# Six PSUM banks for the last attention unit, and another order of loads in the output projection of a conditioned transformer block

## The chip, the cores and the metric

The kernel runs on one core of a Trainium2 chip (trn2). The metric is the device time of one execution in microseconds; smaller is better. Of several runs the median is given. One further execution was profiled, and every time that is placed on an axis here is counted from the start of that profile's span.

## The reference

A transformer block whose normalisations are modulated by a condition vector: x is (2, 2048, 512) in float32, 16 heads of 32, a hidden layer of 2048.

```python
mod = silu(condition) @ Wada + bada
sh_a, sc_a, gt_a, sh_m, sc_m, gt_m = split(mod, 6, axis=1)
xm = layernorm(x, g1, be1) * (1 + sc_a) + sh_a
q, k, v = split_heads(xm @ Wqkv)                    # 16 heads of 32
a = softmax(where(causal, q @ k.T * 32**-0.5, -inf)) @ v
x = x + gt_a * (merge_heads(a) @ Wproj + bproj)
xm = layernorm(x, g2, be2) * (1 + sc_m) + sh_m
x = x + gt_m * (gelu(xm @ W1 + b1) @ W2 + b2)       # exact gelu
```

## The kernel before

The two batches are worked one after the other: modulation, query/key/value products of batch 0, attention of batch 0, output projection of batch 0, query/key/value products of batch 1, attention of batch 1, output projection of batch 1, and last the two-layer perceptron of both batches.

**Attention** goes by units. A unit is a group c of four heads (C is 4 groups) and a block i of 512 queries; a batch has 16 units, and the order of the blocks in the last group is 0, 2, 1, 3 (`last_order`), so the last unit has the most keys. A unit is cut into steps, one for each tile of 128 keys (the last three tiles under the causal mask, which are narrower, share two steps); the last unit has 15 steps. In a step, for each of the four heads:

- TensorE puts minus the row maxima into a PSUM bank (`st`, from `fold` and `sel`), the four heads side by side, and adds the transposed scores (`st`, from `qst` and `kst`); a bank comes from `st_bank()`;
- ScalarE takes the exponential out of the bank into SBUF (`e`, L566), and with that the bank is free;
- two steps later TensorE multiplies `e` by the values (`o`); sums over keys are made by adding pairs and fours of `e` (`ee`, L592, on VectorE in the last unit and on GpSimd otherwise) and by a product with ones (`sm`).

PSUM has eight banks: two of the pool `ps_s` (tag "s": row maxima, gate row and the scores of later units), four of `ps_st` (tag "st"), and one each for `o` and `sm`. In the last unit no later scores are left, so `st_bank` counts its banks (`n_bank`) and takes one in six from "s". In the last unit `prepare` also works ahead for the projection: at step 5 it makes the row of the gate in an "s" bank (`ps_rows`) and copies it to SBUF (L406), then it multiplies the projection's weights and the first block of attention outputs. `prefetch` (step 3) loads the projection's weights, the first two blocks of outputs (`at_s`), the first four token tiles (`xt_s`) and the next stage's first tokens into SBUF that the keys and queries no longer need.

**The output projection** (`project_phase`) goes over 16 tiles of 128 tokens, four for each block in `last_order`; `n` counts them. For a tile:

- SyncE loads its tokens `xt` (L951; the first four are there already), and GpSimd adds the gated bias to them (L952);
- TensorE makes the tile's product over four chunks of 128 (`ps_o`; each chunk is two records in the profile, since they are float32);
- VectorE adds the product to `xt` (L959) and takes its statistics (L204, L205), SyncE stores it (L961);
- VectorE multiplies one chunk of the next block's outputs by their inverse softmax sums (L965), which TensorE needs for the next block's tiles.

The inverse sums come through DRAM: the sums are loaded (`load_sums`, L322), inverted on VectorE (`invert`, L329) and stored (L330), and then loaded spread over the partitions (`widen`, L336, into `wide_d` or straight into SBUF). For the last unit all of that can only be done in the projection. `rb` and `rbs` are the spread inverses, a block each.

Between the tiles, `between(n)` does work of the stage that follows: for batch 0 it loads the weights of the query/key/value products (`load_w`, L758, three transfers of 1 MB from ScalarE's queue) and normalises the first tokens of batch 1 (`norm`); for batch 1 it normalises and transposes tokens for the perceptron (`ln_t`) and adds them up (`token_sums`).

Each engine has a queue of its own and works it in order. A scheduler fills the queues by when it takes an instruction to be ready, earlier than the program's order where it can; `mm(...)` and `act(...)` pin an instruction behind all that was written before it for its engine. Transfers are not pinned. An SBUF pool opened after another was closed lies in the same memory, so its tiles wait until the old ones are done with.

Of the kernel before, what the change touches and what calls it, by code (L numbers as in the profile page):

```python
# [8 lines left out]
F32 = mybir.dt.float32  # L9
# [8 lines left out]
P = 128  # L18
# [3 lines left out]
QB = 512  # L22
# [5 lines left out]
def dit_block_kernel(  # L28
# [35 lines left out]
    nc = tc.nc  # L64
    B, T, D = x.shape
    HID = W1.shape[1]
    C = D // P
    FC = HID // P
    NT = T // P
    HC = P // HD  # L70
    TQ = QB // P
# [11 lines left out]
    def pool(name, bufs=1, **kw):  # L83
        return tc.tile_pool(name=name, bufs=bufs, reuse_waits="tile", **kw)
# [101 lines left out]
    def x_rows(n):  # L186
        t0 = (n % NT) * P
        return x[n // NT, t0 : t0 + P, :]

    def mm(*args, **kw):  # L190

        return tc.keep_in_program_order(nc.tensor.matmul(*args, **kw))  # L192

    def act(ins):

        return tc.keep_in_program_order(ins)
# [5 lines left out]
    def stats(pool_, xt, n, mv):  # L202
        st = pool_.tile([P, 6], F32, tag="stat", name="stat", bufs=2)
        nc.vector.bn_stats(st, xt)  # L204
        nc.vector.bn_aggr(mv[:, n, :], st)  # L205

    def inv_std(mv, rstd, lo, hi):
        nc.scalar.activation(rstd[:, lo:hi], mv[:, lo:hi, 1], AF.Sqrt, bias=eps)
        nc.vector.reciprocal(rstd[:, lo:hi], rstd[:, lo:hi])
# [50 lines left out]
    units = []  # L260
# [4 lines left out]
    last_order = [i for _, i in units[-NQ:]]  # L265
# [249 lines left out]
    def attention_phase(row):  # L515
        b, vv, kst, qst = row.b, row.vv, row.kst, row.qst
        with pool(f"att{b}") as ap, pool(
# [4 lines left out]
            n_bank = [0]  # L522

            def scores_t(u, step, n):

                def st_bank():

                    n_bank[0] += u == len(units) - 1
                    if n_bank[0] % 6 > HC:
                        return ps_sp.tile([P, QB], F32, tag="s", name="st")
                    return ps_stp.tile([P, QB], F32, tag="st", name="st")

                c, i = units[u]  # L540
                tiles = steps_of[u][step]
                q0 = tiles[0][1]
                w = sum(QB - q for _, q in tiles)
                sts, es = [], []
                row.score(max(0, n - 5))
                n = min(n, 5)
                for h in range(HC):
                    g = slice(h * HD, (h + 1) * HD)
                    st = st_bank()
                    mm(  # L550
                        st[:, :w], sel[g, :], fold[u % 2][g, q0 : q0 + w],
                        start=True, stop=False,
                    )
                    sts.append(st)
                for h in range(HC):
                    at = 0
                    for j, q in tiles:
                        mm(
                            sts[h][:, at : at + QB - q],
                            kst[c][:, h, j * P : (j + 1) * P],  # L560
                            qst[u][:, h, q:],
                            start=False, stop=at + QB - q == w,
                        )
                        at += QB - q
                    e = ap.tile([P, QB], F32, tag="e", name="e", bufs=E_BUFS)
                    act(nc.scalar.activation(e[:, :w], sts[h][:, :w], AF.Exp))  # L566
                    if tiles[0][0] >= i * TQ:

                        d = e.rearrange("p (t k) -> p t k", k=P)[:, 0 : TQ : TQ - 1, :]
                        d = d[:, : len(tiles), :]  # L570
                        act(
                            nc.gpsimd.affine_select(  # L572
                                d, d, pattern=[[0, len(tiles)], [1, P]],
                                compare_op=ALU.is_ge, fill=0.0,
                                base=0, channel_multiplier=-1,
                            )
                        )
                    es.append(e)
                    if h >= HC - n:
                        row.score(1, st_bank if h == 2 else None)  # L580
                row.score(n - HC)
                return es
# [61 lines left out]
            def due(u, step):  # L644

                rate, past = 0.0, weight[step]
                for v in range(u + 1, len(units)):

                    left = sum(weight[step : max(step + 1, starts[v] - 3)])
                    rate = max(rate, (cum[v] - row.spent) / left)  # L650
                return row.spent + rate * past

            for u, (c, i) in enumerate(units):
# [5 lines left out]
                for n_step, tiles in enumerate(steps_of[u]):  # L659
                    last = n_step == steps - 1  # L660
                    if n_step == 0:
# [4 lines left out]
                    n = row.count(  # L666
                        due(u, starts[u] + n_step) - QB // 2, u + AHEAD
                    )
# [70 lines left out]
    class Qkv:  # L739
# [20 lines left out]
        def norm(self, g, j):  # L760
# [12 lines left out]
            )  # L773

        def group(self, g, hp, between, among):


# [138 lines left out]
    def project_phase(row, psum, between):  # L916

        b = row.b
        with pool(f"proj{b}") as pp:
            n = 0
            ats = list(row.at_s)
            rbs = {1: row.rb_s[1], 2: row.old_queries()}
            for k, i in enumerate(last_order):
                if k in (0, 1):

                    at = pp.tile([P, C, QB], F32, tag="at", name="at", bufs=2)
                    nc.sync.dma_start(at, od[b][last_order[k + 2]])  # L930
                    ats.append(at)
                at = ats[k]
                for t in range(TQ):

                    if n == 0:
                        rbs[3] = pp.tile([P, C, QB], F32, tag="rb", name="rb")
                        row.load_sums(len(units) - 1, len(units))
                        nc.sync.dma_start(rbs[2], wide_d[b][last_order[2]])
                    elif n == 1:
                        row.invert(len(units) - 1, len(units))  # L940
                        nc.sync.dma_start(
                            rbs[3][:, : C - 1], wide_d[b][last_order[3]][:, : C - 1]
                        )
                    elif n == 2:
                        row.widen(len(units) - 1, rbs[3][:, C - 1, :])
                    nt = b * NT + i * TQ + t
                    if k == 0:
                        xt = row.xt_s[t]
                    else:
                        xt = pp.tile([P, D], F32, tag="xt", name="xt", bufs=4)  # L950
                        nc.sync.dma_start(xt, x_rows(nt))  # L951
                    act(nc.gpsimd.tensor_tensor(xt, xt, bgate, ALU.add))  # L952
                    ps = psum.tile([P, D], F32, tag="mm", name="ps_o")
                    for c in range(C):
                        mm(
                            ps, at[:, c, t * P : (t + 1) * P], row.wproj[:, c, :],
                            start=(c == 0), stop=(c == C - 1),
                        )
                    nc.vector.tensor_tensor(xt, ps, xt, ALU.add)  # L959
                    stats(pp, xt, nt, mv2)  # L960
                    nc.sync.dma_start(x1d[nt], xt)  # L961
                    if k + 1 < NQ:
                        d = ats[k + 1][:, t, :]
                        act(
                            nc.vector.tensor_tensor(d, d, rbs[k + 1][:, t, :], ALU.mult)  # L965
                        )
                    between(n)
                    n += 1
        inv_std(mv2, rstd2, b * NT, (b + 1) * NT)


    row = Row(0)
# [115 lines left out]
    first, row = row, Row(1)  # L1088
    with pool("qkv1") as qp, pool("ps_qkv1", bufs=6, space=PSUM) as ps_mm:
        qkv = Qkv(row, qp, ps_mm)  # L1090
        qkv.xts[0] = first.next_s

        def between(n):
            if n == 2:
                qkv.load_w(nc.scalar)
            if n in (5, 8):
                qkv.norm(0, n // 8)()

        project_phase(first, ps_mm, between)

        def also(g, n):
            if n % 4 == 1:
                quarters.step()

        with pool("hl1") as hp:
            quarters.more_rooms = lambda: [
                hp.tile([P, piece], F32, tag="w7", name="w7", bufs=2)
            ]
            qkv.run(hp, also)
            assert quarters.at >= FC  # L1110
            quarters.store()
# [8 lines left out]
    with ExitStack() as mlp:  # L1120
# [54 lines left out]
        def between(n):  # L1175
# [13 lines left out]
            if n == 13:  # L1189
                token_sums()  # L1190

        project_phase(row, ps_mm, between)
        w7 = [load_w1(f) for f in range(2)]
        bp_cm.__exit__(None, None, None)
# [270 lines left out]
```

## Time and profile before

| | |
|---|---|
| median of three runs | 2526.72 us (2524.92 to 2527.82) |
| the profiled execution | 2526.39 us, its span 2524.7 us |
| busy in the span | PE 2460.4, VectorE 1351.5, GpSimd 982.0, ScalarE 895.1 us |
| last unit of batch 0 (756.9 to 805.2) | 48.30 us, PE busy 48.11, granted clock 1.00 |
| projection of batch 0 (805.2 to 875.7) | 70.50 us, PE busy 61.27, granted clock 0.95 |
| last unit of batch 1 (1603.3 to 1651.6) | 48.30 us, PE busy 48.11, granted clock 1.00 |
| projection of batch 1 (1651.6 to 1713.3) | 61.70 us, PE busy 59.67, granted clock 1.00 |

PE is TensorE's products, PEld its weight loads, DVE is VectorE, ACT ScalarE, POOL GpSimd, SP SyncE; L959 is line 959 of the kernel. A product's end is modelled in the profile, so PE that counts as busy may still be waiting for a bank; the starts are measured, and differences from start to start are the safer reading. A line of a timeline has start, duration, engine, line, operation, what is written from what, tile shapes, count, and in brackets the idle time ahead of it with what ended it. A line of waits has total, times and longest. In both, the part before the colon or bracket names who waited and for what.

### The profile page before, as it was taken

How to read it: one execution, taken by the hardware profiler on the slowest of the kernel's cores; microseconds unless marked ns; L12 is line 12 of the kernel's file. 1: busy time of each engine (PE TensorE's matmuls, PEld its weight loads, DVE VectorE, ACT ScalarE, POOL GpSimd, SP SyncE). 2: the span in 40 equal slices, each digit the busy share in tenths (PEclk: the TensorE clock that was granted, in tenths of full speed). 3: DMA queues.
4: the chain of work that ended last, by engine and by line, in shares of the span. 5: the costliest groups of instructions: out<-in, count | busy, mean ns of one | idle time of the engine just before them, and what ended most of it. 6: DMA issues, size and time to landing. Idle time of an engine off the chain costs nothing.

```text
span 2524.7 us, 30931 instructions
## 1 busy us (share of the span) xinstructions
PE 2460.4 (97%) x10977; PEld 1172.8 (46%) x10977; DVE 1351.5 (54%) x2820; ACT 895.1 (35%) x1667; POOL 982.0 (39%) x1158
## 2 busy tenths in 40 slices
PE   7999999999999899999999999999999999999998
PEld 3445445444444344554444444444444444444443
DVE  3465657667565625656675756665353353344424
ACT  2213455454545011155545454613312312311310
POOL 0062786766772362058767785241101201200200
PEclk9999999999999999999999999999999999999999
DMA  6667123041224596450514113163223233322422
GB/s 221 208 223 193 39 52 84 22 109 43 87 90 141 193 296 200 133 109 22 109 43 93 39 38 134 68 219 119 87 92 132 85 100 108 108 93 72 140 84 96
DMA packets 133445, 285.71 MB, mean 113 GB/s; under 512 B 13301, under 2 KB 42525, under 8 KB 128426
## 3 DMA queue, kind: packets, MB, share of 16 engines
q1 hardware_dynamic: 126226, 257.47, 34.2%
q0 software_dynamic: 5376, 23.07, 2.6%
q10 hardware_dynamic: 1688, 3.19, 0.4%
q8 instruction: 86, 1.41, 0.2%
q14 instruction: 69, 0.57, 0.1%
HBM read 209.76 MB, written 81.79 MB: 115 GB/s over the span
## 4 chain that ended last, share of the span: by engine, by line
PE 61%; DVE 2%; DMA 1%; SPq 1%; issue 0%; ACT 0%; POOL 0%; DVEq 0%; ACTq 0%
PE ps_y L192 15%; PE ps_h L192 15%; PE st L192 9%; PE o L192 5%; PE s L192 4%; PE ps_qk L192 4%; PE ps_o L192 2%; PE sm L192 2%; PE ps_v L192 2%; SPq L336 1%; PE ps_xt L200 1%; DVE junk L436 1%; PE ps_o L200 0%; DVE mx L441 0%; DMA r<-sum 0%
## 5 line engine op out<-in xcount | busy, mean ns | idle before, releaser
L566 ACT ACTIVATE e<-st 128x512 f32<-128x512 f32 (+1 forms) x1152 | 575.3, 576 | 509.4 <-PE st L192 460.5
L441 DVE TENSOR_REDUCE mx<-s 128x1 f32<-128x512 f32 x616 | 413.7, 686 | 273.5 <-PE s L192 272.1
L592 POOL TENSOR_TENSOR ee<-e 128x512 f32<-128x512 f32 x336 | 420.9, 1287 | 246.3 <-ACT e L566 245.7
L192 PE MATMUL s<-kst,qst 128*128 128x512 f32 (+3 forms) x1058 | 453.5, 447 | 17.8 <-DVE mx L436 8.5
L192 PE MATMUL st<-qst,kst 128*128 128x512 f32 (+3 forms) x1280 | 438.1, 392 | 0.0
L192 PE MATMUL o<-e,vv 128*32 128x512 f32 (+3 forms) x2560 | 294.9, 542 | 0.0
L192 PE MATMUL ps_h<-sx,w 128*128 128x512 f32 x640 | 286.7, 592 | 0.0
L436 DVE CUSTOM_DVE_ANT_0 junk<-s,causal 128x384 bf16<-128x384 f32 (+3 forms) x442 | 211.1, 478 | 138.9 <-PE s L192 130.6
L1236 POOL TENSOR_TENSOR c<-c 128x512 f32<-128x512 f32 x32 | 40.6, 1270 | 620.9 <-DVE c L1198 620.9
L192 PE MATMUL ps_y<-sh,w 128*128 128x512 f32 x640 | 277.5, 593 | 0.0
L192 PEld LDWEIGHTS st<-qst,kst 128*128 128x128 f32 x1280 | 230.4, 192 | 88.0 <-issue 63.3
L192 PEld LDWEIGHTS s<-kst,qst 128*128 128x128 f32 x1058 | 199.3, 190 | 144.0 <-issue 47.7
L192 PE MATMUL ps_qk<-xmT,wqkv 128*128 128x512 f32 x512 | 242.3, 601 | 2.2 <-DVE xmT L248 2.2
L572 POOL TENSOR_SCALAR_AFFINE_SELECT e<-e 128x128 f32<-128x128 f32 (+1 forms) x384 | 124.3, 341 | 289.3 <-ACT e L566 282.8
L1198 DVE TENSOR_TENSOR h<-c,ps_h 128x512 f32<-128x512 f32 x128 | 88.0, 687 | 232.5 <-PE ps_h L192 232.5
L592 POOL TENSOR_TENSOR ee<-ee 128x512 f32<-128x512 f32 x168 | 210.8, 1283 | 0.0
L192 PEld LDWEIGHTS ps_h<-sx,w 128*128 128x128 f32 x640 | 121.1, 190 | 150.2 <-issue 149.5
L192 PEld LDWEIGHTS ps_y<-sh,w 128*128 128x128 f32 x640 | 121.1, 191 | 148.3 <-issue 146.9
L192 PE MATMUL st<-fold,sel 32*128 32x512 f32 (+1 forms) x1152 | 156.8, 485 | 2.7 <-DVE fold L500 2.0
L1222 ACT ACTIVATE h<-h,cols 128x512 f32<-128x512 f32 x128 | 92.3, 721 | 182.0 <-DVE h L1198 182.0
L192 PEld LDWEIGHTS st<-fold,sel 32*128 32x128 f32 x1152 | 62.2, 183 | 183.8 <-ACT e L566 124.8
L192 PEld LDWEIGHTS ps_qk<-xmT,wqkv 128*128 128x128 f32 x512 | 95.2, 192 | 98.9 <-issue 91.8
(124 smaller groups left out, 2368.9 us busy)
## 6 DMA issues: line engine op xcount, KB each, us to landing
qst<-q SPq DMA_DIRECT2D x128, 256.0 KB
w<-w1d SPq DMA_DIRECT2D x34, 896.0 KB
w<-w2d SPq DMA_DIRECT2D x28, 1024.0 KB
kst<-k SPq DMA_DIRECT2D x24, 1024.0 KB
q<-hl SPq DMA_DIRECT2D x32, 512.0 KB
k<-hl SPq DMA_DIRECT2D x32, 512.0 KB
kst<-k SPq DMA_DIRECT2D x32, 256.0 KB
w<-in_L_cond_W_dram POOLq DMA_DIRECT2D x64, 128.0 KB, 4.7
```

The costliest lines, as they stand in the source:

```text
L192: return tc.keep_in_program_order(nc.tensor.matmul(*args, **kw))
L200: return tc.keep_in_program_order(nc.tensor.transpose(dst, src, ident[:n, :n]))
L336: nc.sync.dma_start(dst, inv_d[self.b][u].unsqueeze(1).to_broadcast([HC, HD, QB]),)
L436: nc.vector.tensor_tensor_reduce(junk[:, :w], s[:, :w], causal[:, QB - w :], 1.0, MASKED, ALU.add, ALU.max, m,)
L441: nc.vector.tensor_reduce(m, s[:, :w], axis=AX.X, op=ALU.max)
L566: act(nc.scalar.activation(e[:, :w], sts[h][:, :w], AF.Exp))
L572: nc.gpsimd.affine_select(d, d, pattern=[[0, len(tiles)], [1, P]], compare_op=ALU.is_ge, fill=0.0, base=0, channel_multiplier=-1,)
L592: act(engine.tensor_tensor(dst, x, y, ALU.add))
L1198: nc.vector.tensor_tensor(dst, x, y, op)
L1222: nc.scalar.activation(d, d, AF.Gelu, bias=col(r_b1 + chunk, 1))
L1236: nc.gpsimd.tensor_tensor(c1_, c1_, c2_, ALU.subtract)
```

## The change

It has four edits. In `st_bank`, two of six banks of the last unit come from "s" instead of one of six, so that its tiles go round six banks. In `project_phase`, the tokens are loaded by `tokens(upto)` into six buffers instead of four: six tiles ahead of everything else in the phase, and then, at tile n, up to tile n + 5. The spread inverses of the last block go into the buffer of the first block's (`row.rb_s[0]`) instead of one of their own; their first three chunks are loaded at tile 0 instead of 1, the last unit's sums are inverted at tile 3 instead of 1 and spread at tile 4 instead of 2. In batch 0, `load_w` is called at tile 6 instead of 2.

```diff
                     n_bank[0] += u == len(units) - 1
-                    if n_bank[0] % 6 > HC:
+                    if n_bank[0] % 6 >= HC:
                         return ps_sp.tile([P, QB], F32, tag="s", name="st")
                     return ps_stp.tile([P, QB], F32, tag="st", name="st")
...
             n = 0
             ats = list(row.at_s)
-            rbs = {1: row.rb_s[1], 2: row.old_queries()}
+            rbs = {1: row.rb_s[1], 2: row.old_queries(), 3: row.rb_s[0]}
+            rows_x = [b * NT + i * TQ + t for i in last_order for t in range(TQ)]
+            xts = list(row.xt_s)
+
+            def tokens(upto):
+                while len(xts) < min(upto, NT):
+                    xt = pp.tile([P, D], F32, tag="xt", name="xt", bufs=6)
+                    nc.sync.dma_start(xt, x_rows(rows_x[len(xts)]))
+                    xts.append(xt)
+
+            tokens(TQ + 6)
             for k, i in enumerate(last_order):
...
                     if n == 0:
-                        rbs[3] = pp.tile([P, C, QB], F32, tag="rb", name="rb")
                         row.load_sums(len(units) - 1, len(units))
                         nc.sync.dma_start(rbs[2], wide_d[b][last_order[2]])
-                    elif n == 1:
-                        row.invert(len(units) - 1, len(units))
                         nc.sync.dma_start(
                             rbs[3][:, : C - 1], wide_d[b][last_order[3]][:, : C - 1]
                         )
-                    elif n == 2:
+                    elif n == 3:
+                        row.invert(len(units) - 1, len(units))
+                    elif n == 4:
                         row.widen(len(units) - 1, rbs[3][:, C - 1, :])
-                    nt = b * NT + i * TQ + t
-                    if k == 0:
-                        xt = row.xt_s[t]
-                    else:
-                        xt = pp.tile([P, D], F32, tag="xt", name="xt", bufs=4)
-                        nc.sync.dma_start(xt, x_rows(nt))
+
+                    tokens(n + 6)
+                    nt, xt = rows_x[n], xts[n]
                     act(nc.gpsimd.tensor_tensor(xt, xt, bgate, ALU.add))
...
         def between(n):
-            if n == 2:
+            if n == 6:
                 qkv.load_w(nc.scalar)
             if n in (5, 8):
                 qkv.norm(0, n // 8)()
```

## The prediction

> **What bounds the kernel now.** First the busy line of the page: TensorE is the engine to follow.
>
> ```profile
> PE 2460.4 (97%) x10977; PEld 1172.8 (46%) x10977; DVE 1351.5 (54%) x2820; ACT 895.1 (35%) x1667; POOL 982.0 (39%) x1158
> ```
>
> A change that leaves TensorE's work alone can win only the time in which TensorE doesn't run at its pace, so I looked for that in the four stretches that the diff touches. The table by stretches (us, then busy PE, PEld, DVE, ACT, POOL, then granted clock, DMA share, GB/s) shows holes in the two projections: about 3.7, 5.3 and 2.0 us idle, and a clock of 0.75 and 0.90 after the second.
>
> ```profile
> 820.00:830.00 10.00, 6.34 (x15) 2.47 (x15) 6.27 (x15) 0.00 (x0) 0.00 (x0) 1.00 0.91 305
> 840.00:850.00 10.00, 4.74 (x11) 2.22 (x11) 9.04 (x20) 0.30 (x1) 4.35 (x4) 0.75 0.49 153
> 850.00:860.00 10.00, 10.00 (x25) 4.80 (x24) 8.69 (x19) 1.13 (x2) 2.32 (x2) 0.90 0.51 173
> 1680.00:1690.00 10.00, 7.97 (x24) 3.56 (x24) 9.93 (x19) 1.13 (x2) 2.22 (x3) 1.00 0.91 305
> ```
>
> The timeline of PE names who ended each hole of the first projection: always DVE's multiplication by the inverses (L965).
>
> ```profile
> 821.41 1.13 PE L192 MATMUL ps_o<-kst 128*128 128x512 f32 x2 [1.35 <-DVE kst L965]
> 823.53 1.12 PE L192 MATMUL ps_o<-kst 128*128 128x512 f32 x2 [0.99 <-DVE kst L965]
> 825.97 4.56 PE L192 MATMUL ps_o<-kst 128*128 128x512 f32 x10 [1.32 <-DVE kst L965]
> ...
> 844.28 1.33 PE L192 MATMUL ps_o<-kst,at 128*128 128x512 f32 x2 [3.94 <-DVE at L965]
> 846.94 2.08 PE L192 MATMUL ps_o<-kst,at 128*128 128x512 f32 x2 [1.32 <-DVE at L965]
> ```
>
> Why DVE is late, from the waits of 805.2 to 875.8 (total, times, longest): it stood for the last unit's sums, and for a token tile that POOL could not add its bias to.
>
> ```profile
> POOL xt L952 <- DMA xt<-in_x_dram: 41.7, 6, 25.4
> ...
> DVE r L329 <- DMA r<-sum: 6.6, 1, 6.6
> DVE xt L959 <- POOL xt L952: 6.6, 1, 6.6
> ...
> PE ps_o L192 <- DVE at L965: 5.5, 3, 3.9
> ```
>
> Why those loads were late, from SP's timeline: the sums' load is issued 6.4 us after their store, the first token loads of the phase at 824.7.
>
> ```profile
> 805.59 0.32 SPq L619 DMA_DIRECT2D o<-ot  x1
> 806.09 0.53 SPq L618 DMA_DIRECT2D sum<-sums  x1
> 812.14 0.31 SPq L930 DMA_DIRECT2D at<-o  x1
> 812.51 0.42 SPq L322 DMA_DIRECT2D r<-sum  x1
> ...
> 824.73 2.70 SPq L951 DMA_DIRECT2D xt<-in_x_dram  x4
> ```
>
> Meanwhile the 3.1 MB of the next weights, issued by ACT from 805.65 to 808.35, fill the DMA (389 GB/s from 810 to 820): the sums landed at 812.0, their reload at 820.4, the tokens at 832. In the second batch, which loads no such weights, the sums' store to reload takes 1.7 us, and DVE doesn't wait for it.
>
> Last, the last unit (started 756.9 and 1603.3). Four maxima products (fold) take 0.43 us from start to next start when their banks are free; here is one that takes 1.01.
>
> ```profile
> 763.71 0.50 PE L192 MATMUL st<-fold,sel 32*128 32x512 f32 x4
> 764.14 1.20 PE L192 MATMUL st<-qst,kst 128*128 128x512 f32 x4
> ...
> 766.26 1.08 PE L192 MATMUL st<-fold,sel 32*128 32x512 f32 x4
> 767.28 1.20 PE L192 MATMUL st<-qst,kst 128*128 128x512 f32 x4
> ```
>
> **What the skill says.** The Trainium skill, "DMA: Bandwidth & Descriptors", section "Issuing engines are not separate DMA queues": transfers started by scalar, sync or gpsimd run on the same 16 engines and interleave. The trace agrees: ACT's weights delayed SP's 8 KB store. "TensorE: Matmul & The Clock Gate", section "What's actually happening": an idle window of about 3.4 us halves the clock. It agrees: after the 3.94 us hole, eight transposes take 1.71 us instead of 0.87. "GPSIMD Engine Reference", section "Key points": POOL shares its SBUF interfaces with VectorE and hinders VectorE instructions with two SBUF inputs. It agrees: L965 takes 0.66 us alone and up to 1.68 us beside POOL's addition.
>
> **Part 1: six banks.** Before, five of six transposed tiles share four banks, so a tile reuses the bank of four or five tiles earlier. Counted from a step's first score product, its four exponentials end at 1.20, 1.69, 2.18 and 2.67 us (step at 776.1), and the next four fold products start at 2.13. Waiting for the third exponential costs 0.03 to 0.10 us, for the fourth 0.58. I sum start to start over the unit: two of 0.58, and 0.03, 0.09, 0.09, 0.04, 0.09, 0.09: 1.57 us in each batch. With a rotation of six, a tile needs the exponential of six tiles earlier, at the latest the second of the step before (1.69), 0.4 us early: all 1.57 goes. Added is a new wait. The gate row (ps_rows, step 6 of 15) takes one of the two "s" banks, and both now hold that step's second and third tile. It would start 1.12 us after the step's first score product and must wait for 1.69: **0.57 us** on PE, with o's products queued behind it. Bounds: 0 if it gets a free bank, 1.05 if it gets the third tile's. Net 1.0 a batch, **2.0 in both** (1.0 to 3.1).
>
> **Part 2: first projection.** It lasts 805.20 to 875.73, 70.53 us. Its work at full pace: 128 product records at 0.429 us (16 tiles of 3.43) and two groups of transposes of 0.87, with 0.1 for the first: 56.8. The excess of 13.7 is 4.5 (sums), 7.3 (tiles 8 and 9, late tokens), and 2.0 at the lower clock.
>
> The reciprocal moves from tile 1 to tile 3. At full pace DVE is there at about 819; without the weights in the way I expect the sums in at 810 to 812, as in batch 1 (reciprocal run at 1661.0, 9.4 us into the phase, unwaited). The token loads move ahead of everything: six of 256 KB, 1.6 MB, 4 us at 389 GB/s. Some must wait for SBUF in which `ot` and `sums` lie, about as `at` did until 812, and they hold SP's queue for that long; `at` (1.05 MB), the wide inverses (0.8 MB) and the sums' load follow. POOL needs the first token tile at about 821. Each later load waits, at the head of SP, for the store of the tile just done (up to 2.1 us before); with 0.8 us of issuing a cycle is about 3 us against 3.43 for PE, and the lead is five tiles, 17 us. The weights' three DMAs (0.4 us each on ACT) move behind the first pair's activations, to about 832; before, their packets ran until 820.2, 14.6 us after the first issue, so about 847, and the first product that needs it starts near 862. Those are the covers: 8, 9 and 15 us. The inverses of tile 3 load into a buffer that DVE has read by 798.4; the widening moves from tile 2 to 4 and is needed at tile 11.
>
> Late next is DVE itself at the block boundaries. Per tile it works 0.69 + 0.69 + 0.17 + 0.66 = 2.2 us, in all with the norms some 40 us of 57. But the multiplication for the next block's fourth chunk comes 2.2 us after tile 3's last product (3.2 beside POOL), and PE wants it after 2.57. I take 0.4 at each of three boundaries, 1.2 (0 to 1.9). Gain **12.5** (11.8 to 13.7).
>
> **Part 3: second projection.** 1651.63 to 1713.29; the excess beside DVE is 0.97 (transposes waiting for xn) and 1.55 (chunk 3 of tile 8 waiting for L965), both because tile 4's addition was at 1674.9 though PE was ready at 1669. With tokens early, 2.5 less a rest of 0.2: **2.3** (1.0 to 2.5).
>
> **Sum.** 2.0 + 12.5 + 2.3 = 16.8. The profiled execution took 2526.39 (span 2524.70), 0.33 under the median of the runs; 2526.7 - 16.8 = 2509.9: **2510**. What follows each projection starts off TensorE's last product, so the time stays saved. The query/key/value stage after the first has its own hole, at 930 to 937 (2.8 us, then about 1.7 at half clock), which may close or grow as transfers shift: 4.5 us either way, taken as zero.
>
> **Rivals.**
> A, the weights are not later. Queues here are not in program order: bn_stats of the next batch (placed at tile 5) ran at 800, before tile 0's addition. If the weights still leave ACT at once, 6.5 MB is in flight, 16.8 us at 389 GB/s, and the sums land at about 823.5 instead of 819: DVE 4.5 us late at tile 3, PE too. For it: ACT has nothing else to do. Against: in the first projection most DMAs kept about their program order. 2510 + 4.5: **2514.5**.
> B, given back in the next stage: the hole at 930 doubles, 4.5 us, **2514.5**, up to 2519 with A.
> C, slower: SP becomes the chain. Token loads 10 to 15 each stand before the next tile's store; stores landing slowly because the weights now run at that time would stretch the cycle. One store took 7.0 us in the crowd (823.8 to 830.8). At a cycle c, tile 15 is late by 6(c - 3.43) - 17 plus that landing: 16 us at c = 7.8, about the 13.7 and 4.3 of all that could be won, less 2.0 of clock; from there it decides. At c = 9 tile 15 is 23.4 late: 2526.7 - 4.3 - 13.7 + 23.4 + 2.0 = **2534**. Against: DMA carried only 153 to 173 GB/s after 840.
> D, no gain: DVE is the true limit near tile 8 (9.04 and 9.93 of 10 us busy), and early tokens only move the wait. Then the first projection keeps its 7.3 and 2.0 and the second its 2.5; with A the 4.5 stays as well, and only part 1 remains: 2526.7 - 2.0 = **2524.7**. Against: DVE there was catching up, with stretches of 6.27 busy just before.
>
> **How the numbers follow.** Main case 0.55 (2506 to 2513); A 0.18, B 0.13, C 0.07, D 0.07. About 0.2%, 5 us, is what a measurement of this kernel can tell from no change. Faster: main, A, B: 0.86; same: D, 0.07; slower: C, 0.07. The range: 2505 (upper ends of parts 1 and 3, and half of the later hole closed) to 2519 (A with B).
>
> **What would show it.** Right: fold groups all at 0.43; ps_rows waiting about 0.57 on ACT; no DVE wait at L329; POOL's additions of tile 4 before 822; first projection 57 to 59 us at clock 1.00; second 59 to 60. Wrong: weights issued before 812 (A); a new hole near 920 to 940 (B); SP waits at the token loads above 4 us each (C); L965 still ending holes at tile 8 with tokens there (D).

## The result, and the profile after

The kernel after takes **2511.86 us** at the median of four runs (2510.82 to 2515.68), the kernel before, run beside it, 2525.82 (2524.21 to 2527.82): a ratio of 0.994, 95% interval 0.9927 to 0.9952. The profiled execution of after is its slowest run, 2515.68 us with a span of 2514.0, 10.7 under the span of before.

To see where the gain comes from I cut both traces at the first matmul of each stage (all in us; the last column is what the prediction wrote down):

| stretch | before | after | change | predicted |
|---|---|---|---|---|
| last unit, two batches | 48.34 + 48.34 | 47.29 + 47.29 | -2.10 | -2.0 |
| first projection | 70.53 | 65.17 | -5.36 | -12.5 |
| query/key/value stage after it | 198.20 | 195.44 | -2.76 | 0 (4.5 either way) |
| second projection | 61.66 | 60.48 | -1.18 | -2.3 |
| all other stretches | 2097.6 | 2098.3 | +0.7 | 0 |

The total met the forecast of 2510, but not by its sum: the touched stretches gave 11.4, not 16.8, and 2.8 of that came from a stage put down at zero. No edit accounts for the rest: the median of after lies 3.8 below the profiled execution. Stretches that no edit touches differ that much between traces (the first attention stage, to its last unit, from 528.9 to 533.7 over the kernels of this study, the last stage from 810.2 to 813.2), so below I compare the touched stretches, and give each kernel's time beside them. A stretch comes from one profiled execution, and its scatter wasn't measured for each kernel; a projection whose own code is the same took 70.53 in before and 69.24 with the banks alone, so a difference of 1 to 2 us between two projections is no finding by itself. The last unit with six banks lay between 47.27 and 47.30 in every trace.

The busy line first: PE's instructions are as many as before, and TensorE is still the engine to follow.

```profile
PE 2454.5 (98%) x10977; PEld 1170.2 (47%) x10977; DVE 1356.1 (54%) x2820; ACT 895.1 (36%) x1667; POOL 982.9 (39%) x1158
```

The last unit of after in PE's timeline (columns as explained ahead of the prediction):

```profile
771.31 0.51 PE L192 MATMUL st<-fold,sel 32*128 32x512 f32 x4
771.75 1.20 PE L192 MATMUL st<-qst,kst 128*128 128x512 f32 x4
773.42 1.12 PE L192 MATMUL ps_rows<-modr,pick 32*128 32x512 f32 x2 [0.47 <-ACT e L566]
...
775.47 0.51 PE L192 MATMUL st<-fold,sel 32*128 32x512 f32 x4
775.90 0.50 PE L192 MATMUL st<-qst,kst 128*128 128x512 f32 x1
```

Fold groups are 0.43 to 0.44 us from their start to the next start, and `ps_rows` starts 1.67 us after the step's first score product, where the prediction counted 1.12 without a wait: the one added wait.

The stretches of the first projection (columns as before: busy PE, PEld, DVE, ACT, POOL, then granted clock, DMA share, GB/s):

```profile
820.00:830.00 10.00, 4.94 (x8) 1.87 (x7) 5.17 (x11) 0.00 (x0) 2.07 (x2) 0.83 0.90 310
840.00:850.00 10.00, 10.00 (x31) 4.79 (x30) 8.99 (x21) 1.43 (x3) 3.82 (x3) 1.00 0.53 151
850.00:860.00 10.00, 8.96 (x22) 3.83 (x21) 6.86 (x14) 0.00 (x0) 2.53 (x2) 1.00 0.54 176
```

The stretch of the late tokens, 840 to 850, had PE busy for 4.74 of 10 us at a clock of 0.75 and is full now, although DVE is 8.99 us busy: DVE was not the limit. The first stretch, 820 to 830, is worse than before (4.94 us busy against 6.34), and has lost clock. PE's timeline, then the waits (total, times, longest):

```profile
804.10 16.57 PE L192 MATMUL ps_o<-kst 128*128 128x512 f32 x38
825.73 6.25 PE L192 MATMUL ps_o<-kst 128*128 128x512 f32 x10 [5.06 <-DVE kst L971]
...
858.00 11.43 PE L192 MATMUL ps_o<-kst,at 128*128 128x512 f32 x26 [1.04 <-DVE at L971]
```

```profile
POOL xt L958 <- DMA xt<-in_x_dram: 23.8, 5, 14.3
POOL xt L958 <- DMA wqkv<-in_L_cond_Wqkv_dram: 8.8, 1, 8.8
...
DVE r L329 <- DMA r<-sum: 4.0, 1, 4.0
```

One hole of 5.06 us has taken the place of the three short ones, ended by the multiplication by the inverses (L971 here, L965 before), and DVE had stood 4.0 us at the reciprocal for the sums. The cause is in the queues: ACT's and SP's timelines, then what SP's queue itself waited for.

```profile
804.54 0.97 ACTq L758 DMA_DIRECT2D wqkv<-in_L_cond_Wqkv_dram  x2
...
813.73 0.38 ACTq L758 DMA_DIRECT2D wqkv<-in_L_cond_Wqkv_dram  x1
```

```profile
805.25 0.53 SPq L618 DMA_DIRECT2D sum<-sums  x1
805.88 6.42 SPq L932 DMA_DIRECT2D xt<-in_x_dram  x6
812.39 0.38 SPq L940 DMA_DIRECT2D at<-o  x1
815.16 0.33 SPq L322 DMA_DIRECT2D r<-sum  x1
```

```profile
SPq L932 <- DMA sum<-sums: 3.6, 1, 3.6
...
SPq L322 <- DMA xt<-in_x_dram: 2.4, 1, 2.4
```

The weights still leave ACT at the phase's start, two of three at 804.5 and 805: rival A. The six token loads stand ahead of the sums' reload, one of them waits 3.6 us for the store of the sums, whose SBUF it takes over, and the reload waits 2.4 us more for an earlier token load to land. It leaves at 815.16, 11.1 us into the phase (812.51 and 7.3 us in before), and DVE has it at 822.5.

In the second projection the two holes of before are gone and a new one stands at the first block boundary:

```profile
1658.14 1.12 PE L192 MATMUL ps_o<-kst 128*128 128x512 f32 x2 [1.10 <-DVE kst L971]
```

### The profile page after: what moved, and what is told of

The parts are those of the page before. It is cut to its first block, busy times and chain, and to the rows that moved or that the text cites. A ratio compares the mean times of both kernels' runs of the same rounds, so it can differ in the third digit from the quotient of the medians.

```text
span 2514.0 us, 30944 instructions
## 1 busy us (share of the span) xinstructions
PE 2454.5 (98%) x10977; PEld 1170.2 (47%) x10977; DVE 1356.1 (54%) x2820; ACT 895.1 (36%) x1667; POOL 982.9 (39%) x1158
## 4 chain that ended last, share of the span: by engine, by line
PE 61%; DVE 3%; DMA 1%; SPq 1%; issue 1%; ACT 0%; DVEq 0%; ACTq 0%
PE ps_y L192 15%; PE ps_h L192 15%; PE st L192 9%; PE o L192 5%; PE s L192 4%; PE ps_qk L192 4%; PE ps_o L192 3%; PE sm L192 2%; PE ps_v L192 2%; SPq L336 1%; PE ps_xt L200 1%; DVE junk L436 1%; PE ps_o L200 0%; DVE mx L441 0%; DMA r<-sum 0%
```

## The experiments

Three theories were open. **A**: the next weights, in flight with everything else, make the sums late, and the move in the code did not move them. **E**: the order on SP's queue makes them late. **Others**: the later inverses or the banks do more or less than thought. A later theory, **H**, came from the third experiment: DVE stands at statistics of the next stage's tokens that have not landed yet. Each kernel's edit is shown against before or after.

### Banks alone

```diff
# against before
-                    if n_bank[0] % 6 > HC:
+                    if n_bank[0] % 6 >= HC:
```

> The kernel before with only the rotation of six banks. Theory (as predicted): the last unit shrinks from 48.34 to 47.29 us in each batch, fold waits all gone, one wait of about 0.55 us at ps_rows; both projections as before (70.5 and 61.7), total 2.1 us less. Rival: the banks' gain is taken back where the projection starts earlier into the same late sums, so that the first projection grows by about 1 us and the total falls by 1 us or less.

Measured: 2524.44 us (ratio 0.9994, 0.9987 to 1.0001). Last units 47.27 and 47.28, first projection 69.24, second 61.83. The edit is worth its 2.1 us where it stands, and the first projection did not take it back. In the time alone this cannot be told from no change.

### The weights' call back at tile 2

```diff
# against after
-            if n == 6:
+            if n == 2:
                 qkv.load_w(nc.scalar)
```

> The kernel after with the call for the next weights back at tile 2 (as in before), all else kept. Theory A (the call's place does not decide when the weights leave, since ACT's queue has them at its front either way): weights issued at 804 to 814 in both, first projection 65 us within 0.5, no difference in time over 1 us. Rival (the move did delay them in part, the third weight DMA left at 813.7): all three leave by 806, the sums come still later, first projection 1 to 3 us longer than 65.2.

Measured: 2512.54 us (0.9949, 0.9932 to 0.9966); first projection 65.08 against 65.17, next stage 195.23 against 195.44. The first weights leave at 804.0. Moving the call from tile 2 to tile 6 does nothing here: the untied loads go to the front of ACT's queue from either place.

### The weights tied in place

```diff
# against after
-                queue.dma_start(self.w[:, :, f : f + D], w_v[:, :, f : f + D])
+                act(queue.dma_start(self.w[:, :, f : f + D], w_v[:, :, f : f + D]))
# for this call of load_w only; act() ties an instruction behind the one traced before it on its engine
```

> The kernel after with the three loads of the next weights tied behind the instruction that precedes them on ACT in program order (the activations of the first norm pair). Theory A (the weights in the DMA make the sums late): weights leave ACT at 825 to 832, the sums' reload lands by 816, DVE does not wait at the reciprocal, the 5.06 us hole and the slow clock after it go; first projection 65.2 to about 58.3, total about 7 us below after, unless the next stage waits for its weights. Rival E (the six token loads ahead of the sums in SP's queue, and SP's wait for a free DMA slot, make the reload late, and the weights are innocent): the reload is still issued after 815 and lands after 819, a hole of 3 us or more stays, first projection above 62. Rival F (given back): the next stage waits for the late weights and takes the gain.

Measured: 2515.63 us (0.9954, 0.9937 to 0.9971), not below after. The first half of A is right: ACT issues the weights from 832.0, the reload leaves SP 0.5 us after `at` instead of 2.8, and DVE does not wait at the reciprocal; the first 48 products take 21.91 us instead of 27.73. E alone is out with that: the order on SP's queue is unchanged. What that order adds while the weights are in flight was not tested. But the projection is longer, 66.97. PE's timeline, DVE's, and SP's with what it waited for:

```profile
824.80 4.56 PE L192 MATMUL ps_o<-kst 128*128 128x512 f32 x10 [0.94 <-DVE kst L971]
...
860.07 14.35 PE L192 MATMUL ps_o<-kst,at 128*128 128x512 f32 x28 [5.39 <-DVE at L971]
```

```profile
855.00 0.69 DVE L204 BATCH_NORM_STATS2 stat<-x 128x6 f32<-128x512 f32 x1 [5.64 <-DMA x<-in_x_dram]
```

```profile
851.63 0.33 SPq L932 DMA_DIRECT2D xt<-in_x_dram  x1
852.01 0.90 SPq L751 DMA_DIRECT2D x<-in_x_dram  x2
```

```profile
SPq L932 <- DMA x1d<-xt: 21.9, 6, 7.0
```

`x` is not a tile of the projection but a token tile of the next stage, which works its tokens in groups of four tiles; the statistics of these tiles run on DVE ahead of their place in the program. The second group was loaded from 823.7 to 830.6, and its normalizations up to 846.3 freed three of the four buffers of `x`; the tile that DVE stands at is the first of the third group. Its load wasn't slow once it had left: it left at 852.0, and DVE went on at 855.0 (848.6 and 851.5 in after). It left late because it stands on SP's queue behind the projection's token loads, and each of these waits there for the store of a finished tile to land, once for 7.0 us from 836.9, while the weights' packets run (834.2 to 846.3). The longest such wait is 5.9 to 7.4 us in all six kernels of this study with the weights tied, and 2.1 to 3.7 in the eight others. So DVE stands 5.6 us, and the multiplication for tile 12 is queued behind it. That is theory **H**. Rival F does not hold: the next stage takes 195.21. What slows SP is the mechanism of the prediction's rival C (stores that land slowly because the weights run then), but it strikes the next stage's tokens, not the projection's.

### Early tokens alone

```diff
# against before: from the change, only
+            tokens(TQ + 6)
...
+                    tokens(n + 6)
+                    nt, xt = rows_x[n], xts[n]
# and rbs[3] = row.rb_s[0], for room in SBUF; its first three chunks loaded at tile 0, as in after
```

> The kernel before with only the tokens loaded six tiles ahead (and the wide inverses of tile 8 in the buffer that after uses for them, to have room); banks, inverse at tile 1, widening at tile 2, weights called at tile 2 as before. Theory A: the holes at tiles 8 and 9 (7.3 us with the clock's 2.0) go, the wait for the sums stays or grows by the 2 us that their reload is later: first projection 62.5 to 64.5, second 59.5 to 60.5, total 8 to 10 below before. Rival G (the later inverse is what helped, and tokens alone leave DVE waiting at tile 1 with PE behind it for 8 us): first projection 67 or more.

Measured: 2515.7 us (0.9959, 0.9944 to 0.9973); first projection 64.27, next stage 194.63, second projection 60.63. All that the change gains in these three stretches comes with this edit: 10.9 of before's 330.4 us are gone, against 9.3 with the whole change, a difference within the scatter of the stretches. DVE waits 4.9 us at the reciprocal, also as A has it. The shorter next stage comes with this edit too. Its old hole, 2.64 us idle at 933 in before, is 0.63 at 924 in after; why, no run was made to tell.

### The inverses early again

```diff
# against after
-                    elif n == 3:
+                    elif n == 1:
                         row.invert(len(units) - 1, len(units))
-                    elif n == 4:
+                    elif n == 2:
                         row.widen(len(units) - 1, rbs[3][:, C - 1, :])
```

> The kernel after with the last reciprocal back at tile 1 and the widening at tile 2; banks, early tokens, place of the weights' call as in after. Theory (the later reciprocal gains nothing: DVE waits for the same sums, landing at 822 to 823, one or two tiles sooner or later): first projection 63.8 to 65.2, like the 64.27 of the run with tokens alone; second projection as in after; total within 1.5 us of after. Rival (the later inverse lets DVE finish two more tiles before it stands still, which saves PE about 3 us): first projection 67 to 69.

Measured: 2509.79 us (0.9939, 0.992 to 0.9959); first projection 66.59, in neither range; second 60.47. DVE waits 4.2 us at the reciprocal (4.0 in after), and after a hole of 5.08 us PE takes 7.60 us for the next ten records (6.25 in after, 5.94 with early tokens alone). Early inverses gave 64.27 in one kernel and 66.59 in this one, late ones 65.17: what the later inverse is worth, within 2 us, stays open.

### The inverses later still

```diff
# against after
-                    elif n == 3:
+                    elif n == 5:
                         row.invert(len(units) - 1, len(units))
-                    elif n == 4:
+                    elif n == 6:
                         row.widen(len(units) - 1, rbs[3][:, C - 1, :])
```

> The kernel after with the last reciprocal at tile 5 and the widening at tile 6 instead of 3 and 4; weights untouched. Theory A (the sums land at 822 to 823 because of the weights, and DVE's in-order wait for them is the whole of the first hole): at tile 5 DVE is at about 826, does not wait, and the hole of 5.06 us with the slow clock after it goes; first projection 65.2 to 58.5 or 60, the widened row still in time for tile 11. Rival (the late reciprocal only moves the hole: the inverses of the last block come late at tiles 11 and 12): a new hole of 2 us or more before tile 12.

Measured: 2516.23 us (0.996, 0.9946 to 0.9974), first projection 66.77. DVE doesn't wait for the sums any more, and yet PE has a hole of 3.57 us at the same place (and two more, 0.78 and 3.39, at tile 8). A's claim that the wait for the sums is the whole of the hole falls. POOL's and DVE's timelines of this kernel:

```profile
814.04 8.30 POOL L958 TENSOR_TENSOR xt<-xt,bgate 128x512 f32<-128x512 f32 x6 [8.28 <-DMA xt<-in_x_dram]
```

```profile
818.16 1.66 DVE L971 TENSOR_TENSOR kst<-kst,qst 128x512 f32<-128x512 f32 x1
819.74 2.89 DVE L229 TENSOR_SCALAR xn<-qst,mv,rstd 128x512 f32<-128x512 f32 x2
822.55 0.68 DVE L965 TENSOR_TENSOR kst<-ps_o,kst 128x512 f32<-128x512 f32 x1
```

POOL's six additions come in one go from 814, when the first token has landed, and beside them DVE's normalizations take 1.4 us instead of 0.53 and its multiplication 1.66 instead of 0.66. In after the same burst (8.11 us from 813.95) runs while DVE stands. By these figures three normalizations and one multiplication take 3.8 us longer together, which is about the hole. So there seem to be two things behind one hole. That the burst is the second one is read from this trace; no run moved the burst alone. The weights are in both: with them tied and the inverse left at tile 3 (a kernel further down), the burst starts at 809.1 and is over at 817.8, before the multiplication of tile 3.

### All statistics of the next stage tied

```diff
# against after; know(g) = the statistics of group g, tied with act()
+            if n == 3:
+                qkv.know(0)        # in the projection
...
+                        if n == 3:
+                            self.know(g + 1)   # in each group of the stage, both batches
```

> The kernel after with the statistics of the next stage's tokens tied to a place in DVE's order (traced at tile or product 3, two before they are used, both batches) instead of running as soon as the scheduler thinks their tokens are there. Theory H (DVE stands at statistics whose tokens have not landed, and PE's hole before tile 12 and the two in the next stage near 924 and 934 follow from that): these holes go, first projection 65.2 to about 64.2, next stage 195.4 to about 194, the 5.06 us hole at the reciprocal stays; total 2 us below after. Rival I (the statistics only become late where they are tied, and transposes wait for them): holes of 1 to 4 us ahead of transposes, next stage longer than 196.

Measured: 2518.02 us (0.9968, 0.9959 to 0.9976); first projection 68.96, next stage 198.53. The 1.04 us hole before tile 12 goes, as H says, but rival I is right on the rest:

```profile
824.46 6.88 PE L192 MATMUL ps_o<-kst 128*128 128x512 f32 x10 [4.17 <-DVE kst L979]
834.38 1.44 PE L200 MATMUL ps_xt<-ident,xn 128*128 128x128 f32 x8 [3.05 <-DVE xn L229]
```

Statistics that had run at 800 to 812, in DVE's free time, now come from 824 on, behind the wait for the sums, and the transposes wait for them. With the weights tied as well (the same edit on the kernel of "The weights tied in place"):

> Weights tied behind the first norm pair's activations, and the next stage's statistics tied too. Theory A with H: neither the sums nor the next stage's tokens stop DVE; first projection 58 to 59.5 (against 65.2 in after and 67.0 with the weights tied alone), next stage 193 to 196, total 6 to 8 below after. Rival F (the weights that leave at 832 hold the token loads on SP's queue, so that the tokens of the projection itself are late at tiles 11 to 13, or the next stage waits for its weights): a hole of 3 us or more between 845 and 880 stays.

Measured: 2514.92 us (0.9952, 0.9936 to 0.9968); first projection 62.47, next stage 198.82. The stand at tile 12 is gone, the 3.05 us at the transposes is not, and so the projection misses theory A with H's range.

### All statistics tied, with the multiplication first and the gate row earlier

```diff
# against the kernel before it
-            elif n == 5:
+            elif n == 4:
                 ps = rows_of(ps_sp, 0, self.b, "s")
...
+                    # the multiplication of ats[k + 1] by rbs[k + 1] moved here
                     nc.vector.tensor_tensor(xt, ps, xt, ALU.add)
```

> As the one before, and two more edits: in each tile DVE multiplies the next block's chunk before it takes the tile's own product, and the gate row is made one step earlier (step 5 of 15), when its bank has long been read. Theory: the wait of 0.55 us at ps_rows goes (last unit 47.29 to about 46.75 in each batch), the rest of 1.0 to 1.3 us at the block boundaries goes (first projection to about 57.3, second 60.5 to about 59.2); total 8 to 11 below after. Rival (DVE's order pushes the product's addition back, its PSUM bank comes free later): projections longer than in the run before by 0.5 us or more.

Measured: 2510.0 us (0.9938, 0.992 to 0.9956). Last units 46.72 each and second projection 59.08, as expected; first projection 59.69, not the 57.3 expected, with 2.27 us idle left ahead of the transposes; the next stage 200.30, 4.9 more than in after.

### The weights tied, and only the second group's statistics

```diff
# against the kernel with the weights tied in place
+                        if self.row.b and g == 0 and n == 1:
+                            self.know(1)
```

> The kernel after with the weights tied behind the first norm pair's activations, and, of the statistics, only those of the next stage's second group tied (to that stage's first group); the others run as in after. Theory A with H: no wait for the sums, no stand at tokens of the next stage; only 1 to 2 us left at the boundaries: first projection 58 to 59.5, next stage 195 to 197, total 5 to 7 below after. Rival (the stand is at the transfers and comes out elsewhere): a hole of 3 us or more somewhere between 840 and 900.

Measured: **2506.71 us** (2501.73 to 2513.12; ratio 0.9928, 0.9911 to 0.9944). First projection 57.96, next stage 195.52, second projection 60.56: 408.6 us in the touched stretches against 415.7 in after, 7.0 less. A with H holds, and the rival does not: PE's timeline has one idle time in that projection:

```profile
821.78 4.56 PE L192 MATMUL ps_o<-kst 128*128 128x512 f32 x10 [0.78 <-DVE kst L979]
```

and SP's timeline shows the sums' reload going out without waiting:

```profile
806.20 2.92 SPq L940 DMA_DIRECT2D xt<-in_x_dram  x6
809.16 0.43 SPq L948 DMA_DIRECT2D at<-o  x1
809.63 0.43 SPq L322 DMA_DIRECT2D r<-sum  x1
```

The six loads take 2.92 us where they took 6.42. SP still waits for stores at the token loads, up to 6.2 us, but nothing in the projection waits for that: the second group's buffers are now in use until the next stage, so the third group's loads leave only at 883.9, and no statistics of theirs stand in DVE's order before. The intervals of the two ratios to before overlap, so the runs' times alone don't show this version faster than after; the stretches do.

### Only the second group's statistics, with the multiplication first and the gate row earlier

> As the one before, with DVE's multiplication of the next block ahead of the tile's own product, and the gate row a step earlier. Theory: last units 46.7 each, first projection 57 to 57.6, second 59.1, next stage 195 to 197: total about 10 below after, some 2501 to 2503 at the median. Rival (what is won is given back in the next stage, as with all statistics tied, 200.3): next stage above 198.

Measured: 2511.08 us (0.9943, 0.9931 to 0.9954). First projection 56.79, second 59.08, last units 46.71 and 46.72: as expected or a little better, and PE without a hole from 803 to 860.

```profile
803.00:860.00 57.00, 57.00 (x146) 26.17 (x145) 38.37 (x74) 3.84 (x6) 16.70 (x13) 1.00 0.73 239
```

But the rival is right: the next stage takes 200.85, 5.3 more than in the kernel before it. Its PE timeline and its waits there:

```profile
918.13 0.69 PE L192 MATMUL s<-kst,qst 128*128 128x384 f32 x1 [4.50 <-DVE mx L436]
```

```profile
DVE stat L204 <- DMA x<-in_x_dram: 6.3, 3, 2.6
```

It is the hole that stood at 933 in before, 2.64 us there, and 1.62 in the kernel before this one; the maxima come late on DVE, which has stood at statistics of later groups' tokens. Here it is followed by five products at half clock. So a gain of 3.8 in the other four stretches met a loss of 5.3 in the stage between. The stand alone doesn't explain the loss: such waits add up to 6.3 us in this stage and to 5.4 in the kernel before it. Why they cost PE more here, no run tells.

### Before, with only the weights and the second group's statistics tied

> The kernel before with only the next weights tied behind the first norm pair's activations and the second group's statistics tied; banks, tokens and inverses as before. Theory A (the weights in the DMA caused both the late sums and the late tokens): sums' reload lands by 813, DVE does not wait at the reciprocal, the token loads leave by 818, first projection 70.5 to 59 to 62, so that the early tokens were hardly needed. Rival (the tokens are late by their place on SP's queue, weights or not): the hole of 3 us or more at tile 8 stays, first projection 64 or more.

The edit is that of the kernel with only the second group's statistics tied, made on before; the tied call of `load_w` stands at tile 6 here too.

Measured: 2511.11 us (0.9948, 0.9932 to 0.9965). First projection **58.35**, better than expected: without early tokens and with the old inverses it loses both of its old stalls, and DVE does not wait at the reciprocal. SP's timeline:

```profile
806.75 0.42 SPq L322 DMA_DIRECT2D r<-sum  x1
...
818.85 1.89 SPq L959 DMA_DIRECT2D xt<-in_x_dram  x4
```

The reload leaves 2.2 us after the store, the tokens at 818.9 instead of 824.7. In the first batch, the weights were the cause of the late sums and of the late tokens. The statistics tied with them have no part in that: the reload and the tokens leave SP before the first token of that group is loaded, at 820.8. The next stage took 200.90, with the hole at its maxima at 4.10 us. The second projection, where no such weights are loaded, stays at 61.69: there the early tokens are what gains.

## Why the prediction was right or wrong

**Part 1, right to a tenth.** 1.05 a batch against 1.0, the added wait 0.55 against 0.57; making the gate row a step earlier removed it (47.29 to 46.72).

**Part 2, right on what was to be won, wrong on two steps of how.** Of the excess of 13.7, the holes at tiles 8 and 9 and the low clock after them went, as written (8.8 us from start to start), and rival D fell with them. The step that failed is "The weights' three DMAs move behind the first pair's activations, to about 832". They did not move: the place of a call in the program was taken for the place of its transfers in the queue. Rival A's working gave the sums at 823.5 and DVE 4.5 us late, and 822.5 and 4.0 were measured. A was short by the clock: after 5.06 us idle PE ran ten records in 6.25 us, and in 4.56 with the weights tied, so another 1.7. With 1.04 before tile 12 that is 7.8 of the 8.4 us by which the projection still exceeds the 56.8 of its work. DVE's wait for the sums is not all of that hole, as the run with the inverses later still shows.

The second step is the cover "15 us" for the weights, counted to the first product that needs them. With the weights leaving at 832, the projection took 66.97: while they run, stores land late, SP stands up to 7.0 us at its token loads, the next stage's loads leave late behind these, and statistics of those tokens stand in DVE's order ahead of work that PE waits for. Rival C had the first half of this, and looked only at the projection's own tiles. I had read that DVE's order isn't the program's (the statistics at 800), used it for rival A, and didn't ask which others had moved up. With the weights at 832 and the second group's statistics tied, 57.96 was measured; 70.53 - 12.5 is 58.03. So the sum of part 2 was right for a kernel that the change did not make.

**Part 3, the right holes and the wrong rest.** Both holes of before went, 2.5 us. The term that was mis-sized is "a rest of 0.2": it measures 1.3, at the first block boundary, where I had priced the same thing in part 2 at 0.4. The early tokens seem to bring it: POOL adds the bias to six tiles in one go (8.40 us from 1644.79), and beside that a normalization takes 1.49 us and a multiplication 1.44 on DVE, in the tiles ahead of the boundary, where the kernel before had no addition; no run moved the additions alone. With the multiplication ahead of the tile's own product the hole was gone (60.44 to 59.08, the kernels with all statistics tied).

**The stage after** lay within the 4.5 either way, on the good side, 2.8. In other kernels of this study the same stage took 194.6 to 200.9. A hole in that stage can thus grow as rival B has it, though not with this change. C did not show in after, where the weights had not moved (SP's longest wait at a token load 3.3 us, against 4 in its sign); with the weights tied that wait was there, but PE lost nothing to the projection's own token tiles.

**The total** of 2510 against 2511.86 is partly luck. The run is rival A's, for which 2514.5 was written; the touched stretches fell 5.4 us short of the sum, even with the 2.8 from a stage put down at zero, and scatter that no edit explains covered 3.4 of it.

## What to carry to other kernels

Moving a call that starts a transfer doesn't move the transfer if nothing ties it: look in the queue's timeline where it leaves now, and tie it if the gain rests on it. When a stall waits for a small load, ask first which large load is in flight beside it; here, delaying 3.1 MB, with one group's statistics tied, did in the first projection what early tokens and late inverses did not. And before a large transfer is delayed, list all that will be in flight then, with everything queued behind each of their waits, the next stage's early work included.

## What the runs showed of the hardware

A load can wait at the head of its queue for an older, unrelated transfer to land: the sums' reload stood 2.4 us for a token load in after. In that trace the transfers of SP and ACT count on eight semaphores, each used again and again, and these two share one: as far as the trace shows, that is what the reload waits for. A large load delays the stores beside it: SP's longest wait for a store, at the token loads, was 5.9 to 7.4 us in the six kernels in which the 3.1 MB of weights ran at that time, and 2.1 to 3.7 in the eight in which they had run before. DVE is slowed beside POOL in operations with one SBUF tensor too: normalizations (L229) took 0.53 us alone, 1.44 each beside POOL's additions. And a hole can cost more than its length: 5.06 us of idle PE took 1.7 us of clock with it in after, one of 5.08 us some 3.0 where the early inverses were tried again (7.60 against 4.56 us for the next ten records). Its length alone doesn't tell: after the 3.57 us with the inverses later still, ten records took the full-pace 4.56, and after the 2.64 us at 933 in before, four products ran at half pace (0.81 to 0.85 us from start to start).
